# A cross-attention block on one core: the order of the last two blocks' steps, and which queue reads their inverse sums

## The chip, the core and the metric

The kernel runs on one core of one Trainium2 chip. A core has a tensor engine (PE, with its weight loads PEld), a vector engine (VectorE, DVE), a scalar engine (ScalarE, ACT), a general engine (GpSimd, POOL) and a sync engine (SyncE, SP), which issues most of the DMA transfers. Each engine works through its own instructions in the order of the program; engines wait for each other through semaphores. The metric is the device time of one execution in microseconds (us), as the median over runs.

## The reference

Sixteen pairs of an input `x` (1024 x 512) and a context (64 x 512) go through one cross-attention with a residual, all in float32. Cut to what matters:

```python
xq  = (1 + scale_q) * layernorm(x) + bias_q          # scale, bias from silu(cond) @ Wss
xkv = (1 + scale_kv) * layernorm(ctx) + bias_kv
q = (xq @ Wq + bq).reshape(B, Lq, 16, 32)
k, v = split(xkv @ Wkv + bkv)
attn = softmax(q @ k^T / sqrt(32))
out  = (attn @ v).reshape(B, Lq, 512)
return x + (out @ Wp + bp)
```

The part that matters here is the end of it: softmax, its product with `v`, and the projection by `Wp` with the residual.

## The kernel before

The rows of `x` are cut into NB = 32 blocks of 512 rows, two for each of the 16 inputs. Every block goes through the same stages, and the stages of several blocks are interleaved by hand: the program is a list of small steps, and the order of that list is the order on every engine (`manual_schedule`). Lines 1001 to 1221 bring the pipeline in, the loop from line 1224 runs blocks 4 to 29, and lines 1319 to 1413 are the way out, with y = 30 and z = 31.

For block i the steps are these:

- `scores` (L674): the products of queries and keys, in two halves of the keys, and their maxima on VectorE (L698) and copies to SBUF on ScalarE (L707).
- `maxima` and `subtract` (L734, L740): the maximum of each row is spread over a 128 x 2048 tile and taken off on Pool (L742), once for each half.
- `weights` (L746): the exponential on ScalarE (L748), in place, once for each half.
- The row sums. Up to block 30 Pool adds both halves (`total`) and VectorE sums (`row_total`, L791). Block 31 has no such addition: `sums` (L750) sums each half on VectorE (L753), and `halves_total` (L799) puts both together (L720).
- `inverse_rows` (L803): the reciprocal of the sums on VectorE (L806), a write of it to DRAM (`ltd`, L809) and four reads back (`vr`, L811), one for each group of 32 partitions. The detour changes which partition holds which row. All five transfers are issued by SP.
- `spread_rows` (L814): a transpose on VectorE (L817) that repeats each inverse sum over a 128 x 2048 tile, `vb`.
- `mix` (L839): the weights times the values on the tensor engine (L855), into two PSUM tiles of two banks.
- `divided` (L822): the result times `vb`, on VectorE, in two instructions for blocks that use the product scheme below (L835), into the tile `ot`.
- The projection by `Wp`. Block 29 does it plainly (`project`, L879, and `projected`, L893, which adds the residual and stores). All others do it with seven half-size products instead of eight. `row_sums` (L940) makes the four sums and differences of `ot` that this needs on Pool: s1 (L945, for product 5), the difference for product 7 (L946, written over a part of `ot`), s2 (L949, for product 6) and the sum for product 4 (L950, written over a part of `ot`). `product(i, n)` (L952, matmuls at L970) runs product n, eight matmuls, into a PSUM bank; `added(i, n)` (L979) adds the bank to the residual tile `r` on VectorE (L994, for block 31 L989) and stores where a part is complete.

The PSUM banks set the order around the change. The products of block 30 use banks 2 and 3, with product 2 in bank 1; those of block 31 use banks 0 and 1, with product 2 in bank 3 (`acc_bank`, L921). Products of a block add up in their bank, and `added` reads it between them, so the next product in a bank waits for the addition before it. Before the first product, `biased(i, k)` (L927) copies the projection's bias into the bank on ScalarE (L933), and for this the bank's last reader must be done: for `biased(z, 2)` that is `projected(y - 1, 3)`, for `biased(z, 3)` it is `added(y, 2)`.

The order by hand in the way out, from the last exponentials on:

```python
row_sums(y, 0)
project(y - 1, 3, later=True)
sums(z, 0)
projected(y - 1, 3)
biased(z, 2)
product(y, 1); added(y, 1)
weights(z, 1)
product(y, 2); added(y, 2)
biased(z, 3)
row_sums(y, 1)
sums(z, 1); halves_total(z); inverse_rows(z)
```

(written here with several steps on one line). After it come products 7, 6, 4 and 5 of block 30 with their additions, then `mix(z)`, `spread_rows(z)`, product 3 of block 30, `divided(z)`, `row_sums(z, 0)`, products 1 and 2 of block 31, `row_sums(z, 1)`, and products 6, 7, 5, 4 and 3 of block 31.

Of the kernel before, what the change touches and what calls it, by code (L numbers as in the profile page):

```python
# [9 lines left out]
F32 = mybir.dt.float32  # L10
AF = mybir.ActivationFunctionType
ALU = mybir.AluOpType
# [3 lines left out]
P = 128  # L16
# [4 lines left out]
def cross_attention_block(  # L21
# [51 lines left out]
    nc = tc.nc  # L73
# [10 lines left out]
    NB = B * BPB  # L84
# [661 lines left out]
    def weights(i, z):  # L746
        p = s_tiles[i, z]
        nc.scalar.activation(p, p, AF.Exp, scale=SCALE)  # L748
# [54 lines left out]
    def inverse_rows(i):  # L803

        lt = lt_tiles.pop(i)
        nc.vector.reciprocal(lt, lt)  # L806
        v = small.tile([P, NC, NJ], F32, tag="vr", name=f"vr_{i}")
        d = dram.tile([NC, 32, HPC, NJ], F32, tag="lt", name=f"ltd_{i}")
        nc.sync.dma_start(d.rearrange("c a r j -> (c a) r j"), lt)  # L809
        for r in range(HPC):  # L810
            nc.sync.dma_start(v[32 * r : 32 * r + 32], d[:, :, r, :].rearrange("c a j -> a c j"))  # L811
        vt_rows[i] = v

    def spread_rows(i):  # L814
# [78 lines left out]
    def projected(i, t):  # L893
        r = r_tiles[i]
        nc.vector.tensor_add(r[:, t, :], pp_tiles.pop((i, t)), r[:, t, :])
        nc.sync.dma_start(rows_of(out, i)[:, t, :], r[:, t, :])
        if t == NT - 1:
            r_tiles.pop(i)
# [28 lines left out]
    def biased(i, k):  # L927

        b = b_first if k == 2 else b_diff
        k = acc_bank(i, 1 if k == 2 else 7)  # L930
        acc[k] = bank(f"pp_{i}_{k}", k)
        b = b.unsqueeze(1).to_broadcast([P, 2, HO])
        nc.scalar.copy(acc[k].rearrange("p (t h) -> p t h", t=2), b)  # L933

    s1_tiles, s2_tiles = {}, {}

    def half_rows(i, m, k):
        return ot_tiles[i][:, k * HC : (k + 1) * HC, m * HT : (m + 1) * HT]

    def row_sums(i, n):  # L940

        tt = nc.gpsimd.tensor_tensor
        if n == 0:
            s1_tiles[i] = opool.tile([P, HC, HT], F32, tag="s1", name=f"s1_{i}")
            tt(s1_tiles[i], half_rows(i, 1, 0), half_rows(i, 0, 0), ALU.subtract)  # L945
            tt(half_rows(i, 1, 0), half_rows(i, 1, 1), half_rows(i, 1, 0), ALU.subtract)  # L946
        else:
            s2_tiles[i] = opool.tile([P, HC, HT], F32, tag="s2", name=f"s2_{i}")
            tt(s2_tiles[i], half_rows(i, 1, 1), s1_tiles[i], ALU.subtract)  # L949
            tt(half_rows(i, 0, 1), half_rows(i, 0, 1), s2_tiles[i], ALU.subtract)  # L950

    def product(i, n):  # L952

        rows, cols = {
            1: (lambda: half_rows(i, 0, 0), half_weights(0, 0)),
            2: (lambda: half_rows(i, 0, 1), half_weights(1, 0)),
            3: (lambda: half_rows(i, 1, 1), WT[:, 3]),
            4: (lambda: half_rows(i, 0, 1), half_weights(1, 1)),
            5: (lambda: s1_tiles.pop(i), WT[:, 0]),
            6: (lambda: s2_tiles.pop(i), WT[:, 1]),  # L960
            7: (lambda: half_rows(i, 1, 0), WT[:, 2]),
        }[n]
        rows = rows()
        k = acc_bank(i, n)
        if n == 2:
            acc[k] = bank(f"pp_{i}_{n}", k)
        for t in range(2):
            for c in range(HC):

                nc.tensor.matmul(  # L970
                    acc[k][:, t * HO : (t + 1) * HO],
                    lhsT=rows[:, c, t * P : (t + 1) * P],
                    rhs=cols[:, c, :],
                    start=n == 2 and t == 0 and c == 0,
                    stop=c == HC - 1,
                    skip_group_check=True,
                )

    def added(i, n):  # L979

        m, o = {1: (0, 0), 2: (0, 0), 6: (0, 1), 7: (1, 1), 5: (1, 1), 4: (0, 1), 3: (1, 0)}[n]
        r = r_tiles[i][:, 2 * m : 2 * m + 2, o * HO : (o + 1) * HO]
        k = acc_bank(i, n)
        a = acc[k].rearrange("p (t h) -> p t h", t=2)
        if i == NB - 1:

            for ts in ((0,), (1,)) if n == 3 else ((0, 1),):
                ts = slice(ts[0], ts[-1] + 1)
                nc.vector.tensor_add(r[:, ts, :], a[:, ts, :], r[:, ts, :])  # L989
                if n in (2, 3, 4, 5):  # L990
                    dst = rows_of(out, i)[:, 2 * m : 2 * m + 2, o * HO : (o + 1) * HO]
                    nc.sync.dma_start(dst[:, ts, :], r[:, ts, :])
            return
        nc.vector.tensor_add(r, a, r)  # L994
        if n in (3, 4):
            nc.sync.dma_start(
                rows_of(out, i)[:, 2 * m : 2 * m + 2, :], r_tiles[i][:, 2 * m : 2 * m + 2, :]
            )
# [87 lines left out]
    queries(2, 3)  # L1086
    weights(1, 0)
    queries(3, 0, later=True)
    row_sums(0, 0)
    q_stats(4, (0, 1))  # L1090
    sums(1, 0)
    q_stats(4, (2, 3), kvb=2)
# [1 line left out]
    product(0, 1)  # L1094
    added(0, 1)
    product(0, 2)
    row_sums(0, 1)
    q_scale(4, kvb=2)
    query_weight_sums()

# [34 lines left out]
    divided(1)  # L1135
    context_hidden(2)
    queries(3, 3)
    row_sums(1, 0)
    context_features(2)
    q_stats(5, (0, 1, 2))  # L1140
    product(1, 1)
# [1 line left out]
    product(1, 2)  # L1143
    added(1, 2)
    biased(1, 3)
    row_sums(1, 1)
    q_stats(5, (3,))
    q_scale(5)
    row_total(2)
# [32 lines left out]
    turn(5, range(NT))  # L1182
    load_x(7)
    q_scale(6)
    row_sums(2, 0)
    move(5)
    query_product(4, 6)
    weights(3, 0)
# [9 lines left out]
    query_product(4, 7)  # L1198
    query_out(4, 7)
    biased(2, 3)  # L1200
    row_sums(2, 1)
    key_products(2, spare("pk_2"))
    hidden(6, range(NT))
    query_product(4, 5)
# [19 lines left out]
    for i in range(4, NB - 2):  # L1224
        a, b, n, f = i - 1, i - 2, i + 1, i + 2
        kvb = i // 4 * 2 + 2
        kv = i % 4 if kvb < B else None
        if kv == 0:
            load_context(kvb)
        scores(i, 0, crossed=True)  # L1230
        product(b, 6)
        added(b, 6)
        query_product(n, 1)
        query_seed(n)
        added(b, 7)
        scores(i, 1)
        product(b, 5)
        added(b, 5)
        maxima(i)
        subtract(i)  # L1240
        product(b, 4)
        if i + 3 < NB:
            hidden(i + 3, (0, 1, 2))
        query_product(n, 2)
        query_out(n, 2)
        product(b, 3)
        spread_rows(a)
        if i + 3 < NB:
            hidden(i + 3, (3,))
        added(b, 4)  # L1250
        added(b, 3)
        biased(a, 2)
        load_residual(i)
        mix(a)
        divided(a)
        row_sums(a, 0)
        query_product(n, 6)
        weights(i, 0)
        query_out(n, 6)
        if kv == 1:  # L1260
            context_hidden(kvb)
        scale_features(f, (0, 1))
        product(a, 1)
        if i + 4 < NB:
            q_stats(i + 4, (0,))
        added(a, 1)
        product(a, 2)
        if i + 4 < NB:
            q_stats(i + 4, (1,))
        added(a, 2)  # L1270
        weights(i, 1)
        total(i)
        query_product(n, 7)
        query_out(n, 7)
        biased(a, 3)
        scale_features(f, (2, 3))
        row_sums(a, 1)
        if kv == 1:
            context_scaled(kvb)
        if kv == 2:  # L1280
            key_products(kvb, spare(f"pk_{kvb}"))
        if kv == 3:
            value_products(kvb, spare(f"pv_{kvb}"))
        if i + 3 < NB:
            turn(i + 3, range(NT))
        if i + 5 < NB:
            load_x(i + 5)
        elif i == NB - 3:
            load_residual(NB - 1)
        query_product(n, 5)  # L1290
        query_added(n, 5)
        if i + 4 < NB:
            q_stats(i + 4, (2,))
        if kv == 1:
            context_scale(kvb)
        if kv == 2:
            key_tiles(kvb)
        if kv == 3:
            value_tiles(kvb)
        query_product(n, 4)  # L1300
        query_added(n, 4)
        if i + 4 < NB:
            q_stats(i + 4, (3,), kvb=kvb if kv == 0 else None)
        query_product(n, 3)
        query_out(n, 3)
        feature_sums(f)
        product(a, 7)
        row_total(i)
        inverse_rows(i)
        if i + 3 < NB:  # L1310
            move(i + 3)
        if i + 4 < NB:
            q_scale(i + 4, kvb=kvb if kv == 0 else None)
        if kv == 1:
            context_shift(kvb)
# [3 lines left out]
    y, z = NB - 2, NB - 1  # L1319
# [47 lines left out]
    spread_rows(y)  # L1367
    projected(y - 1, 2)
    divided(y)
    row_sums(y, 0)  # L1370
    project(y - 1, 3, later=True)
    sums(z, 0)
    projected(y - 1, 3)
    biased(z, 2)
    product(y, 1)
    added(y, 1)
    weights(z, 1)
    product(y, 2)
    added(y, 2)
    biased(z, 3)  # L1380
    row_sums(y, 1)
    sums(z, 1)
    halves_total(z)
    inverse_rows(z)
    product(y, 7)
    added(y, 7)
    product(y, 6)
# [6 lines left out]
    spread_rows(z)  # L1394
    product(y, 3)
    divided(z)
    row_sums(z, 0)
    added(y, 3)
    product(z, 1)
    added(z, 1)  # L1400
    product(z, 2)
    added(z, 2)
    row_sums(z, 1)
    product(z, 6)
    added(z, 6)
    product(z, 7)
# [47 lines left out]
```

## Time and profile before

| | |
|---|---|
| median of three runs | 1044.82 us (1042.91, 1044.82, 1045.44) |
| the profiled execution | 1045.25 us |
| its span, first to last instruction | 1043.3 us |
| busy: PE, DVE, POOL, ACT | 98%, 82%, 75%, 59% of the span |
| mean granted clock of the tensor engine | 0.998 |

The span is what the profile's times refer to; the execution's own time is 1.95 us longer. By stretches of the span:

| us from the start | what runs | PE busy | DVE busy | ACT busy | POOL busy |
|---|---|---|---|---|---|
| 0 to 26 | way in | 15.5 | 13.3 | 9.4 | 0.7 |
| 26 to 1011 | the blocks | 979.5 | 823.0 | 598.5 | 770.2 |
| 1011 to 1043.3 | the way out that the change touches | 26.8 | 18.1 | 3.0 | 10.6 |

In the third stretch no engine is busy all the time: there it is waits that count, not shares. Rows of a timeline read so: start and length in us, engine, line, operation, what it writes and reads with shapes, how many instructions are merged, and in brackets how long the engine had been idle and what ended that idle time.

### The profile page before, as it was taken

Reading aid. Unit: us, or ns where it says so; the run is one execution under the profiler, and the core shown is the slowest. Engines: PE = TensorE matmul, PEld = TensorE weight load, DVE = VectorE, ACT = ScalarE, POOL = GpSimd, SP = SyncE. Lnnn points to the kernel's source line nnn. Section 1 sums busy time; section 2 is a strip of 40 time slices with the busy share of each in tenths; the row PEclk is TensorE's granted clock in tenths of the full one; section 3 lists DMA queues with packets and bytes.
Section 4 is the critical chain, followed back from the end, with each engine's and each line's share of the span. In section 5 each row is a group of like instructions: output and inputs, shape, how many; then the busy total and the mean of one; then the engine's idle time right before and its main releaser. Section 6 shows DMA issues by size and latency. Waiting matters only on the chain.

```text
span 1043.3 us, 22968 instructions
## 1 busy us (share of the span) xinstructions
PE 1021.9 (98%) x9058; PEld 760.0 (73%) x9058; DVE 854.4 (82%) x1159; ACT 610.9 (59%) x945; POOL 781.5 (75%) x502
## 2 busy tenths in 40 slices
PE   5999999999999999999999999999999999999998
PEld 3635686778777777777777787778787778777746
DVE  5798977987788977987878878898778997776795
ACT  3666755665567655766556666567557665565530
POOL 0479795887868868888668986688876886977861
PEclk9999999999999999999999999999999999999999
DMA  9851555444454434554335454344354444335122
GB/s 341 250 162 54 150 180 154 128 136 139 154 156 143 125 117 140 166 164 132 117 112 161 154 159 133 110 139 155 137 163 118 141 141 131 102 123 161 45 87 84
DMA packets 103499, 147.63 MB, mean 142 GB/s; under 512 B 33464, under 2 KB 34640, under 8 KB 103392
## 3 DMA queue, kind: packets, MB, share of 16 engines
q1 hardware_dynamic: 102368, 144.08, 43.5%
q0 software_dynamic: 1024, 2.10, 0.9%
q8 instruction: 71, 1.16, 0.5%
q14 instruction: 36, 0.29, 0.1%
HBM read 79.02 MB, written 34.60 MB: 109 GB/s over the span
## 4 chain that ended last, share of the span: by engine, by line
PE 91%; DVE 5%; DMA 1%; ACT 1%; POOL 1%; issue 1%; SPq 0%; DVEq 0%; ACTq 0%; POOLq 0%
PE pp L970 35%; PE pq L633 33%; PE po L855 6%; PE ps L681 6%; PE pq L546 4%; PE pv L434 3%; PE pk L398 3%; DVE m L698 1%; DMA x<-in_x_dram 1%; DVE bs L263 1%; DVE ht L503 0%; POOL s L742 0%; DVE lt L791 0%; ACT s L748 0%; DVE l L753 0%
## 5 line engine op out<-in xcount | busy, mean ns | idle before, releaser
L742 POOL TENSOR_TENSOR s<-s,mb 128x2048 f32<-128x2048 f32 x62 | 281.3, 4564 | 171.3 <-DVE mb L729 167.2
L707 ACT COPY s<-ps 128x1024 f32<-128x1024 f32 x128 | 129.4, 1012 | 112.7 <-DVE m L698 69.5
L698 DVE TRANSPOSE_TENSOR_REDUCE m<-ps 128x32 f32<-128x1024 f32 x128 | 150.8, 1215 | 31.1 <-PE ps L681 29.5
L970 PE MATMUL pp<-w_p_sb,ot 128*128 128x256 f32 x744 | 171.0, 379 | 0.9 <-DVE ot L835 0.5
L994 DVE TENSOR_TENSOR r<-pp,r 128x512 f32<-128x512 f32 x210 | 136.3, 670 | 32.1 <-PE pp L970 25.0
L663 ACT ACTIVATE qt<-pq,bias_t 128x256 f32<-128x256 f32 x224 | 92.6, 464 | 116.0 <-PE pq L633 113.3
L970 PEld LDWEIGHTS pp<-w_p_sb,ot 128*128 128x128 f32 x744 | 141.0, 190 | 21.8 <-issue 1.7
L748 ACT ACTIVATE s<-s 128x2048 f32<-128x2048 f32 x64 | 122.3, 1911 | 41.8 <-POOL s L742 40.0
L786 POOL TENSOR_TENSOR sum<-s,s 128x2048 f32<-128x2048 f32 x30 | 136.2, 4541 | 5.5 <-ACT s L748 5.5
L970 PEld LDWEIGHTS pp<-WT,s 128*128 128x128 f32 x496 | 90.6, 191 | 57.0 <-issue 35.2
L970 PE MATMUL pp<-WT,s 128*128 128x256 f32 x496 | 124.2, 394 | 0.2 <-POOL s L949 0.2
L970 PE MATMUL pp<-WT,ot 128*128 128x256 f32 x496 | 117.6, 380 | 1.0 <-POOL ot L946 0.6
L633 PE MATMUL pq<-xt_sums,wq_sums 128*128 128x256 f32 x448 | 108.5, 385 | 0.0
L633 PEld LDWEIGHTS pq<-xt_sums,wq_sums 128*128 128x128 f32 x448 | 82.9, 190 | 32.8 <-issue 21.8
L633 PE MATMUL pq<-xt,wq_sums 128*128 128x256 f32 x448 | 106.6, 381 | 0.0
L633 PE MATMUL pq<-xt,w_q_sb 128*128 128x256 f32 x448 | 106.0, 379 | 0.3 <-ACT pq L645 0.3
L970 PEld LDWEIGHTS pp<-WT,ot 128*128 128x128 f32 x496 | 93.9, 190 | 16.6 <-POOL ot L946 2.3
L324 ACT ACTIVATE x<-x,rstdq 128x512 f32<-128x512 f32 x128 | 96.6, 807 | 1.9 <-DVE rstdq L294 1.9
L670 DVE TENSOR_TENSOR qt<-pq,qt 128x256 f32<-128x256 f32 x112 | 42.0, 417 | 66.5 <-PE pq L633 66.1
L633 PEld LDWEIGHTS pq<-xt,w_q_sb 128*128 128x128 f32 x448 | 85.0, 190 | 13.1 <-ACT xt L573 0.8
L263 DVE BATCH_NORM_STATS2 bs<-x 128x6 f32<-128x512 f32 x128 | 86.9, 679 | 7.3 <-DMA x<-in_x_dram 7.3
L633 PEld LDWEIGHTS pq<-xt,wq_sums 128*128 128x128 f32 x448 | 83.5, 190 | 11.9 <-issue 1.4
(128 smaller groups left out, 1583.4 us busy)
## 6 DMA issues: line engine op xcount, KB each, us to landing
x<-in_x_dram SPq DMA_DIRECT2D x32, 1024.0 KB, 5.9
r<-in_x_dram SPq DMA_DIRECT2D x32, 1024.0 KB, 5.5
out_dram<-r SPq DMA_DIRECT2D x60, 512.0 KB, 3.7
xt<-ht SPq DMA_DIRECT2D x464, 64.0 KB, 2.0
wss_q<-in_L_xcond_Wss_q_dram SPq DMA_DIRECT2D x2, 1024.0 KB, 9.1
ctx<-in_ctx_dram SPq DMA_DIRECT2D x8, 256.0 KB, 3.1
wss_kv<-in_L_xcond_Wss_kv_dram SPq DMA_DIRECT2D x2, 1024.0 KB
w_kv_sb<-in_L_xcond_Wkv_dram SPq DMA_DIRECT2D x1, 2048.0 KB
```

The source lines that it names most:

```text
L263: nc.vector.bn_stats(bs, r)
L324: nc.scalar.activation(dst, src, AF.Identity, bias=rstd[:, 1, j : j + 1], scale=rstd[:, 0, j : j + 1])
L633: nc.tensor.matmul(qa[k][:, m * HT : (m + 1) * HT].rearrange("p (g n) -> p g n", g=2), lhsT=a[:, c, m * P : (m + 1) * P], rhs=x[:, :, c, : ...
L663: nc.scalar.activation(dst, src, AF.Identity, bias=bq_t[:, o : o + 1])
L681: nc.tensor.matmul(pss[r // 2][32 * c : 32 * c + 32, r % 2, :], lhsT=kt[rows, c, z * HK : (z + 1) * HK], rhs=qt[rows, c, :], start=True, s ...
L698: nc.vector.tensor_reduce(m_tiles[i][:, z, 2 * e : 2 * e + 2, :], pss[e].rearrange("p r (j a) -> p r j a", a=32), AX.X, ALU.max, apply_tra ...
L707: nc.scalar.copy(s_sb[:, 2 * e : 2 * e + 2, :], pss[e])
L742: eng.tensor_tensor(s_tiles[i, z], s_tiles[i, z], mb_tiles[i], ALU.subtract)
L748: nc.scalar.activation(p, p, AF.Exp, scale=SCALE)
L786: nc.gpsimd.tensor_tensor(t, s_tiles[i, 0], s_tiles[i, 1], ALU.add)
L970: nc.tensor.matmul(acc[k][:, t * HO : (t + 1) * HO], lhsT=rows[:, c, t * P : (t + 1) * P], rhs=cols[:, c, :], start=n == 2 and t == 0 and ...
L994: nc.vector.tensor_add(r, a, r)
```

## The change

Five things change, all in the last two blocks:

1. In block 31, `weights(z, 1)` comes before `biased(z, 2)` in the list, so before the bias copy on ScalarE.
2. `added(y, 2)` and `biased(z, 3)` go from before `row_sums(y, 1)` to behind `inverse_rows(z)`. The addition of block 30's product 2 so stands behind the sums and the reciprocal of block 31 on VectorE, and ahead of `added(y, 7)`.
3. Of the four reads of block 31's inverse sums, the second and fourth are issued by Pool instead of SP.
4. `row_sums` takes a tuple of steps, each named by the product that it serves. For block 30 the difference for product 7 now comes before s1 (7, 1, then 6, 4). Since s1 reads the part of `ot` that the difference used to overwrite, the difference gets a tile of its own there, in a buffer of the pool `qpool` (tag "wq").
5. For block 31 s2 comes before the difference for product 7: (1, 6), then (7, 4). All other blocks keep (1, 7), then (6, 4), which is the order of before.

```diff
         for r in range(HPC):
-            nc.sync.dma_start(v[32 * r : 32 * r + 32], d[:, :, r, :].rearrange("c a j -> a c j"))
+            (nc.gpsimd if i == NB - 1 and r % 2 else nc.sync).dma_start(
+                v[32 * r : 32 * r + 32], d[:, :, r, :].rearrange("c a j -> a c j")
+            )
...
-    def row_sums(i, n):
+    def row_sums(i, steps):
         tt = nc.gpsimd.tensor_tensor
...
+        for n in steps:
+            if n == 1:
+                s1_tiles[i] = opool.tile([P, HC, HT], F32, tag="s1", name=f"s1_{i}")
+                tt(s1_tiles[i], half_rows(i, 1, 0), half_rows(i, 0, 0), ALU.subtract)
+            elif n == 7:
+                d_tiles[i] = half_rows(i, 1, 0)
+                if i == NB - 2:
+                    d_tiles[i] = qpool.tile([P, 4, HC, HT], F32, tag="wq", name=f"d_{i}")[:, 0]
+                tt(d_tiles[i], half_rows(i, 1, 1), half_rows(i, 1, 0), ALU.subtract)
+            elif n == 6:
+                s2_tiles[i] = opool.tile([P, HC, HT], F32, tag="s2", name=f"s2_{i}")
+                tt(s2_tiles[i], half_rows(i, 1, 1), s1_tiles[i], ALU.subtract)
+            else:
+                tt(half_rows(i, 0, 1), half_rows(i, 0, 1), s2_tiles[i], ALU.subtract)
...
-            7: (lambda: half_rows(i, 1, 0), WT[:, 2]),
+            7: (lambda: d_tiles.pop(i), WT[:, 2]),
...
     divided(y)
-    row_sums(y, 0)
+    row_sums(y, (7, 1))
     project(y - 1, 3, later=True)
     sums(z, 0)
     projected(y - 1, 3)
+    weights(z, 1)
     biased(z, 2)
     product(y, 1)
     added(y, 1)
-    weights(z, 1)
     product(y, 2)
-    added(y, 2)
-    biased(z, 3)
-    row_sums(y, 1)
+    row_sums(y, (6, 4))
     sums(z, 1)
     halves_total(z)
     inverse_rows(z)
+    added(y, 2)
+    biased(z, 3)
     product(y, 7)
...
     divided(z)
-    row_sums(z, 0)
+    row_sums(z, (1, 6))
     added(y, 3)
     product(z, 1)
     added(z, 1)
     product(z, 2)
     added(z, 2)
-    row_sums(z, 1)
+    row_sums(z, (7, 4))
```

## Prediction

> **What bounds the kernel now.** I read the page's share of the ending chain by engine, then that chain in order of time for the last 80 us, then the timeline of the last 70 us. The page gives the whole kernel to the tensor engine: it is busy 98% of the span and holds 91% of the chain. The diff leaves the loop over blocks 4 to 29 with the same instructions in the same order (the steps of `row_sums` are only renumbered, 0 to (1, 7) and 1 to (6, 4)), so only the end, from about 1011 us on, can move. There the chain leaves the tensor engine (columns: start, length, engine, tile, line):
>
> ```profile
> 1011.94 0.59 ACT pp L933
> 1012.53 1.85 ACT s L748
> 1014.38 0.02 issue
> 1014.40 2.32 DVE l L753
> ...
> 1017.07 0.56 DVE lt L806
> ...
> 1017.65 1.44 DMA ltd<-lt
> ...
> 1021.10 1.80 DMA vr<-ltd
> ...
> 1023.02 2.32 DVE vb L817
> ...
> 1025.44 1.24 DVE ot L835
> ...
> 1029.36 1.23 POOL s L949
> 1030.59 0.04 issue
> 1030.64 8.91 PE pp L970 x40
> ```
>
> This is block 31's way out: last exponential, row sums, their inverses through DRAM (`ltd`) and back (`vr`), their spreading, the division, the Pool sums, 40 matmuls, the last output. The reader is to see that each link looks as if a saving there were a saving at the end. The timeline shows how close the runners-up are:
>
> ```profile
> 1002.48 9.07 POOL L742 TENSOR_TENSOR s<-s,mb 128x2048 f32<-128x2048 f32 x2 [8.63 <-DVE mb L729]
> ...
> 1013.62 0.69 DVE L994 TENSOR_TENSOR r<-pp,r 128x512 f32<-128x512 f32 x1 [1.03 <-PE pp L970]
> ...
> 1017.54 1.22 DVE L994 TENSOR_TENSOR r<-pp,r 128x512 f32<-128x512 f32 x2
> ...
> 1018.32 1.96 PE L970 MATMUL pp<-w_p_sb,ot 128*128 128x256 f32 x8 [0.40 <-DVE r L994]
> ...
> 1021.94 2.35 PE L855 MATMUL po<-s,vt 32*32 32x512 f32 x64
> ...
> 1022.05 0.69 DVE L994 TENSOR_TENSOR r<-pp,r 128x512 f32<-128x512 f32 x1 [1.04 <-PE pp L970]
> ...
> 1023.02 2.31 DVE L817 STREAM_TRANSPOSE vb<-vr 128x2048 f32<-128x2048 f32 x1 [0.28 <-DMA vr<-ltd]
> ...
> 1026.71 3.72 PE L970 MATMUL pp<-w_p_sb,ot 128*128 128x256 f32 x16 [0.50 <-DVE ot L835]
> ```
>
> The line that decides is the transpose of L817: VectorE waited only 0.28 us for the DMA. Just before it, in program order, stands `added(y, 5)` (1022.05), which waits for a product of block 30. However early the inverse sums land, the transpose can't pass that addition.
>
> **1. Bias copy behind the exponential.** Pool's second subtraction ends at 1002.48 + 9.07 = 1011.55. ScalarE then has the exponential's data, but stands in `biased(z, 2)`, which waits for an addition until 1011.94; the exponential follows at 1012.47. Changed, it starts at 1011.57 and ends at 1013.49 (0.02 + 1.92), against 1014.38: 0.89 earlier. The copy's reader is product(31, 1), at 1026.71, more than ten us away: cost nothing. `biased(z, 3)` now waits for the later `added(y, 2)` (about 1017.3); nothing is queued behind it on ScalarE, and its reader, product(31, 7), comes after 1031.
>
> **2. The addition behind sums and inverse.** `added(y, 2)` ran at 1013.62 to 1014.31, in the gap before the sums: it cost nothing there, but at the new time of the sums (1013.51) it would hold them until 1014.25. Moved behind the reciprocal, it frees the sums: 1013.51 + 2.32 = 1015.83, half totals 1016.15, reciprocal 1016.73 (0.30 and 0.56 from the chain, 0.02 between). Before, the write to DRAM started at 1017.65; now at 1016.75: 0.90 gained. The price is on VectorE: the addition (0.69, of which about 0.61 counts when one follows the other, since two took 1.22) now stands ahead of `added(y, 7)`. That addition was issued at 1017.54 and is now at 1016.65 + 0.61 = 1017.26. It frees the bank that product(30, 4) waited for at 1018.32, so the tensor engine gains 1017.54 - 1017.26 = **0.28 us**, not 0.90. Products 4 and 5 of block 30 and block 31's mix follow without a gap: `added(y, 5)` moves from 1022.05 to 1021.77, and is done at about 1022.4.
>
> **3. Two queues.** The write lands 1.44 after its issue: 1018.19, plus 0.02. On SP alone the four reads took 1019.11 to 1022.90 = 3.79 us (third issue 1.10, last landing 1.80 after issue), so they would land at 1022.0, already before 1022.4. With two on SP the second is issued near 1018.6 and lands by 1020.4. So the split buys nothing as long as the other two, on Pool, land by 1022.3, 4.1 us after the write. No read of 64-byte pieces was ever issued by Pool; the nearest rows are block 2's feature moves:
>
> ```profile
> 68.08 3.98 POOL L516 DMA_DIRECT2D xt<-ht  x8
> ...
> xt<-ht POOLq DMA_DIRECT2D x8, 64.0 KB, 2.0
> ```
>
> That is 0.50 us per issue and 2.0 from issue to landing: 0.5 + 2.0 = 2.5 us, landing at 1020.7. Those moves have 32 packets each, these reads some 144 (576 small packets for four in the DMA answer for 1018.9 to 1023.1). If Pool's issue grows by 128 data packets over 32, it is 2.0 us each, and with landing 2.0 after the end of the second issue 2 x 2.0 + 2.0 = 6.0 us: 1024.2, 1.9 later than needed. The lower end is a hidden transfer, since VectorE can't start earlier. I take hidden: on SP the same reads cost less per issue than the 32-packet moves (0.42 against 0.59), so here packets don't set the issue time, and between the ends the 0.50 row is the only row of Pool's own. The Trainium skill speaks against this edit: "DMA: Bandwidth & Descriptors", "Issuing engine by pattern", puts simple loads on the hardware path, and its latency list gives about 1 us to first byte from GpSimd against 0.6. By that rule the Pool landings are 0.4 later than SP's 1.8, an estimate of 0.5 + 2.2 = 2.7 us; by the row 2.5. The trace shows both kinds of move landing in 2.0, so no gap of that size at 64 KB. Either way the landing is inside 4.1, and the sum doesn't change. Queued behind the Pool issues is block 31's first row sum, which waits for the division at 1026 anyway; on SP the next is an output store.
>
> **4. Block 30's order (7, 1), with d in its own buffer.** Pool starts at 1011.5 with the difference for product 7, so product 7 can start near 1013.5 instead of 1014.20. But product 4 waits for VectorE until 1018.0, and products 7 and 6 (1.73 each) were done before that in either order. Gain 0. The new buffer's last readers ended at about 986: no wait.
>
> **5. Block 31's order (1, 6, 7, 4).** The transpose now starts at 1022.42 instead of 1023.02, so the division's first half starts at 1024.84 and ends at 1026.05 (mix(31) starts 0.28 earlier at 1021.66 and has its first half by 1023.5: no new wait). That is **0.60** on this stretch, 0.28 from part 2 and 0.32 from the removed DMA wait and its handover. Product(31, 1) then starts at 1026.11. Before, product 6 waited until 1030.64 for the third Pool sum (L949). Now s2 is the second one: s1 1026.14 to 1027.42, s2 after the second half (1027.19) to 1028.75. Products 1 and 2, 16 matmuls at 1.73 us per eight, last until 1026.11 + 3.46 = 1029.57. Product 6 starts there instead of at 1030.64. **1.07 us** in all, of which 0.47 is this order. The difference for product 7 is there at 1030.1, needed at 1031.3.
>
> **Sum.** -0.28 - 0.32 - 0.47 = -1.07 us on the profiled execution's span of 1043.3 (1045.25 with what lies around it), so about 1042.2 and 1044.2. Taken off the median of the three runs, 1044.82, this is **1043.8**: 0.1% less. About 0.3% (3.1 us) is what a measurement of this kernel can tell from no change; so I forecast no change.
>
> **Rivals.**
> A. The forecast, 1043.8: chance 0.56.
> B. All links of the chain add up: 0.90 for the inverse, 3.79 - 2.3 = 1.5 for the split reads, 0.47 for the order: -2.87, 1041.95. For it speaks the chain, where all three are links. Against it: `added(y, 5)` stands before the transpose on VectorE, and the mix ends behind the same products. Chance 0.14, as modelled matmul ends may hide some slack.
> C. The additions behind the reciprocal take everything back except the Pool order, or the order finds the same wait in VectorE's second half: between 0 and -0.5, 1044.6. Chance 0.12.
> D. Slower: the reads on Pool. At 2.0 us per issue they land at 1024.2, the transpose starts 1.9 late, and -1.07 becomes +0.8: **1045.7**. It decides from a landing at about 1023.4, 5.2 us after the write; to be slower by 0.3% it needs 8.3 us, some 3.1 per issue. For it: packets four times as many, a queue unused since 147 us. Against: SP's issues don't grow with packets. One more danger belongs here: the skill's "SBUF — State Buffer", section "SBUF: two separate sides", has a VectorE copy in its two-port mode lock GpSimd out of descriptor writing. In 1018 to 1022 VectorE runs additions with one operand in PSUM; by the rule none blocks, and no run here shows such a block. Chance 0.18.
>
> A beyond noise and half of B give 0.10 for faster by over 0.3%; half of D, where the price is past its worked-out bound, and some noise give 0.10 for slower; 0.80 within. The runs before spread over 2.5 us, so the range is 1042.0 to 1046.0: it holds B's and D's times and leaves less than 2 in 10 outside.
>
> **What would show it.** The second exponential of block 31 starting at 1011.6 and the write of the inverse at 1016.8 (parts 1 and 2); the wait of L817 no longer on a DMA but directly behind an addition (part 3); a POOL row for the reads, near 0.5 us each; product 4 of block 30 still waiting for VectorE near 1018.0 (parts 2 and 4); the 40 last matmuls starting about 1.1 earlier, with no wait for L949's successor (part 5). Wrong it would be if L817 waits for a DMA issued by Pool, or if the time before 1011 differs between the two profiles by more than the tail.

## The result, and the profile after

The changed kernel takes 1042.43 us (median of 22 runs, 1041.30 to 1044.54) against 1045.09 (22 runs) for the one before. The ratio is 0.9983, with a 95% interval of 0.9975 to 0.9991: some 0.9 to 2.6 us less, within the 0.3% band that was forecast as no change. The forecast of 1043.8 was a ratio of 0.9990, inside that interval. The number alone, though, lies nearer to rival B's 1041.95 than to 1043.8, so it takes the profiles to tell the two apart. In a second comparison on another occasion (12 runs against 23) the ratio was 0.9988, interval 0.9977 to 0.9999.

The two profiled executions differ by more than that: their spans are 1043.3 and 1040.5, 2.8 us apart. Most of it is not the change. The third-last column of the view by stretches is the granted clock of the tensor engine. Before:

```profile
159.00:161.00 2.00, 2.00 (x18) 0.75 (x19) 1.00 (x1) 0.54 (x1) 1.74 (x5) 0.66 0.58 184
161.00:163.00 2.00, 2.00 (x6) 1.62 (x5) 1.25 (x1) 1.39 (x2) 0.31 (x2) 0.50 1.02 363
```

and in the changed kernel:

```profile
159.00:161.00 2.00, 2.00 (x22) 1.16 (x7) 0.78 (x2) 1.13 (x2) 1.36 (x5) 1.00 0.58 210
161.00:163.00 2.00, 2.00 (x11) 1.77 (x10) 2.00 (x3) 0.80 (x1) 0.00 (x0) 1.00 1.06 382
```

In the profiled execution of before the clock fell to 0.66 and 0.50 (means of 2 us each). 0.34 x 2 + 0.50 x 2 is 1.7 us of lost clock, and the subtractions on Pool, which stood 0.31 us apart in the two traces at 130 us, stand 1.96 apart at 172. This drop comes in some executions of either kernel and not in others, so spans can't be compared directly. From here on I use the **tail**: the time from the start of block 31's first subtraction on Pool (L742) to the end of the span. It was 1043.3 - 1002.48 = 40.82 before and is 1040.5 - 1000.69 = **39.81** now: 1.01 us less, where the forecast's sum was 1.07. Spans are given to 0.1 us, so a tail is good to about 0.05. Times called "in the tail" count from that start.

The timeline of the changed kernel, with the rows that answer to those shown of before (the lines of the code have moved: L820 is the transpose of L817, L981 the products of L970, L1005 the additions of L994):

```profile
1000.69 9.05 POOL L742 TENSOR_TENSOR s<-s,mb 128x2048 f32<-128x2048 f32 x2 [8.64 <-DVE mb L729]
...
1009.77 1.91 ACT L748 ACTIVATE s<-s 128x2048 f32<-128x2048 f32 x1 [2.59 <-POOL s L742]
...
1014.86 1.82 DVE L1005 TENSOR_TENSOR r<-pp,r 128x512 f32<-128x512 f32 x3
1014.97 0.33 SPq L809 DMA_DIRECT2D ltd<-lt  x1
...
1016.23 1.97 PE L981 MATMUL pp<-w_p_sb,ot 128*128 128x256 f32 x8 [0.62 <-DVE r L1005]
1016.42 0.80 SPq L812 DMA_DIRECT2D vr<-ltd  x2
1016.69 1.17 POOL L812 DMA_DIRECT2D vr<-ltd  x2 [1.79 <-DMA ltd<-lt]
...
1019.96 0.69 DVE L1005 TENSOR_TENSOR r<-pp,r 128x512 f32<-128x512 f32 x1 [1.03 <-PE pp L981]
...
1020.56 2.30 DVE L820 STREAM_TRANSPOSE vb<-vr 128x2048 f32<-128x2048 f32 x1
...
1024.34 3.69 PE L981 MATMUL pp<-w_p_sb,ot 128*128 128x256 f32 x16 [0.22 <-DVE ot L838]
...
1027.87 1.89 PE L981 MATMUL pp<-WT,s 128*128 128x256 f32 x8
```

The exponential starts when Pool's subtraction ends. Three additions now follow the reciprocal in one row (1.82 us for three), and product 4 of block 30 still waits for VectorE, 0.62 us. The transpose has no bracket: it follows the addition before it, which ends at 1020.65. The last row, block 31's product 6, has none either: it follows products 1 and 2 directly. The chain in order of time now reads

```profile
1016.69 0.59 POOL vr L812
1017.28 2.89 DMA vr<-ltd
1020.17 0.04 DVEq L820
1020.21 0.36 issue
1020.56 2.31 DVE vb L820
...
1024.34 12.34 PE pp L981 x56
```

It still runs through Pool's read, but that is not the wait: the read was in at 1020.17, and the 0.36 us of "issue" behind it is time in which VectorE worked on the addition. The last link is 56 matmuls in one piece, where before it was 40, with Pool's third sum ahead of them.

### The profile page after: what moved, and what is told of

Same layout as the page of the kernel before. It is cut to its first block, busy times and chain, and to the rows that moved or that the text cites. A ratio compares the mean times of both kernels' runs of the same rounds, so it can differ in the third digit from the quotient of the medians.

```text
span 1040.5 us, 22970 instructions
## 1 busy us (share of the span) xinstructions
PE 1019.7 (98%) x9058; PEld 760.2 (73%) x9058; DVE 854.2 (82%) x1159; ACT 610.7 (59%) x945; POOL 782.1 (75%) x504
## 3 DMA queue, kind: packets, MB, share of 16 engines
q1 hardware_dynamic: 102080, 144.06, 43.2%
q0 software_dynamic: 1088, 2.12, 0.9%
## 4 chain that ended last, share of the span: by engine, by line
PE 88%; DMA 4%; DVE 4%; ACT 1%; POOL 1%; SPq 1%; issue 1%; DVEq 0%; ACTq 0%; POOLq 0%
PE pp L981 35%; PE pq L633 33%; PE po L858 6%; PE ps L681 6%; PE pv L434 2%; PE pq L546 2%; PE pk L398 2%; DMA x<-in_x_dram 2%; DMA b_p_sb<-in_L_xcond_bp_dram 1%; POOL s L742 1%; DVE m L698 1%; DMA r<-in_x_dram 1%; DVE ht L503 0%; DVE lt L791 0%; SPq L516 0%
## 5 line engine op out<-in xcount | busy, mean ns | idle before, releaser
L742 POOL TENSOR_TENSOR s<-s,mb 128x2048 f32<-128x2048 f32 x62 | 281.2, 4559 | 170.7 <-DVE mb L729 166.6
L981 PE MATMUL pp<-w_p_sb,ot 128*128 128x256 f32 x744 | 171.0, 380 | 0.8 <-DVE r L1005 0.6
L1005 DVE TENSOR_TENSOR r<-pp,r 128x512 f32<-128x512 f32 x210 | 136.2, 670 | 30.4 <-PE pp L981 24.9
L981 PEld LDWEIGHTS pp<-w_p_sb,ot 128*128 128x128 f32 x744 | 141.3, 190 | 21.4 <-issue 2.5
L981 PEld LDWEIGHTS pp<-WT,s 128*128 128x128 f32 x496 | 89.9, 190 | 56.0 <-issue 33.2
L981 PE MATMUL pp<-WT,s 128*128 128x256 f32 x496 | 122.9, 391 | 0.1
L981 PE MATMUL pp<-WT,ot 128*128 128x256 f32 x488 | 115.6, 380 | 0.4 <-ACT pp L936 0.4
L981 PEld LDWEIGHTS pp<-WT,ot 128*128 128x128 f32 x488 | 92.6, 190 | 15.3 <-POOL ot L956 1.3
```

Source lines behind the costliest of these rows:

```text
L742: eng.tensor_tensor(s_tiles[i, z], s_tiles[i, z], mb_tiles[i], ALU.subtract)
L981: nc.tensor.matmul(acc[k][:, t * HO : (t + 1) * HO], lhsT=rows[:, c, t * P : (t + 1) * P], rhs=cols[:, c, :], start=n == 2 and t == 0 and ...
```

## The experiments

Each entry quotes what was expected before the run. All but the last two are a single profiled execution, so differences of 0.1 us in the tail say little. "Product 6" is the start of block 31's product 6 in the tail: 28.16 before, 27.18 changed. It is steadier than the tail, since after it come the same 40 matmuls and the last store, which took 12.54 to 12.81 us over all runs, the changed kernel's included.

### All four reads on SP again

```diff
-            (nc.gpsimd if i == NB - 1 and r % 2 else nc.sync).dma_start(
+            nc.sync.dma_start(
```

> The changed kernel with all four reads of block 31's inverse sums on SP again. 'Tail' is the time from the start of block 31's first subtraction on Pool (L742) to the end of the span: 40.82 us before, 39.81 changed. Theory (the split is hidden behind the addition of block 30's product 5): tail 39.8, within 0.1, and the transpose into vb still starts directly behind that addition. Rival B (the split is worth its full length on SP): tail 41.0 or more.

Tail 39.76, product 6 at 27.22: as with two queues. In the timeline:

```profile
1021.53 0.69 DVE L1005 TENSOR_TENSOR r<-pp,r 128x512 f32<-128x512 f32 x1 [1.04 <-PE pp L981]
1022.14 2.31 DVE L820 STREAM_TRANSPOSE vb<-vr 128x2048 f32<-128x2048 f32 x1
```

The transpose stands directly behind the addition of product 5. The split buys nothing here, because the earlier inverse has already hidden the reads; but only just, since they landed 4.0 us after the write, 0.12 us before the transpose (before, where it waited for them, that distance was 0.12 too).

### The split alone, on the kernel before

```diff
-            nc.sync.dma_start(
+            (nc.gpsimd if i == NB - 1 and r % 2 else nc.sync).dma_start(
```

> The kernel before with the split reads alone (second and fourth read on Pool). Tail before 40.82 us, from the start of block 31's first subtraction to the end. The prediction's price of Pool's reads (0.5 per issue, 2.0 to landing) puts them 0.9 ahead of need, and the transpose starts behind the addition of product 5: tail 40.5. The price that the changed kernel's trace shows (0.28 to begin, 0.59 per issue, 2.9 from the end of the second issue to landing: 3.76 in all) equals SP's 3.79 for four: tail 40.8, with the transpose waiting for Pool's read. Rival B (full value of the split): tail 39.3.

Tail 40.61, product 6 at 27.80: 0.36 earlier in the tail. The transpose, which before waited 0.28 us for the DMA, stands directly behind the addition; the reads took 3.5 us here and landed 0.08 us before it starts. So the split has a value where the reads are late, and that value is the 0.3 to 0.4 us up to the next wait, not 1.5. It was the same 0.3 that parts 1 and 2 take by another way, so it can be had once.

### The exponential alone, on the kernel before

```diff
+    weights(z, 1)
     biased(z, 2)
     product(y, 1)
     added(y, 1)
-    weights(z, 1)
```

> The kernel before with the last exponential alone moved ahead of the bias copy; the addition of block 30's product 2 stays ahead of the sums. Theory: the exponential ends 0.89 earlier, but the sums then wait for that addition (until 1014.25 of the profile before, instead of 1014.40), so all behind it gains 0.15: tail 40.65 (40.82 before). Rival B (a saving at a link of the chain is a saving at the end): tail 39.9.

Tail 40.86: no gain at all, although the exponential ended 0.9 earlier in the tail. The timeline shows both waits that took it:

```profile
1013.27 0.69 DVE L994 TENSOR_TENSOR r<-pp,r 128x512 f32<-128x512 f32 x1 [1.03 <-PE pp L970]
1013.88 2.30 DVE L753 TRANSPOSE_TENSOR_REDUCE l<-s 128x64 f32<-128x2048 f32 x1
...
1022.77 2.31 DVE L817 STREAM_TRANSPOSE vb<-vr 128x2048 f32<-128x2048 f32 x1 [0.56 <-DMA vr<-ltd]
```

The sums follow the addition, not the exponential. The remaining 0.2 us (the write at 14.98 in the tail instead of 15.17) went to the reads, which landed 0.3 us later after the write than in the profile of before.

### Exponential and addition together, on the kernel before

```diff
-    added(y, 2)
-    biased(z, 3)
     row_sums(y, 1)
     sums(z, 1)
     halves_total(z)
     inverse_rows(z)
+    added(y, 2)
+    biased(z, 3)
```

(besides the edit of the run before)

> The kernel before with the last exponential moved and the addition of block 30's product 2 behind the inverse (parts 1 and 2), all four reads on SP and the old Pool orders. Theory: the inverse is 0.9 earlier, product 4 of block 30 only 0.28, and the transpose, now behind the addition of product 5, 0.6 to 0.67: tail 40.15 to 40.25. Rival B: tail 39.9. Rival C (taken back by the addition in front of product 7's): tail 40.5 to 40.8.

Tail 40.10, product 6 at 27.50. Parts 1 and 2 alone give 0.72 of the 1.01 us (0.66 at product 6), with the reads on SP and the old orders on Pool. The exponential alone gave nothing; the next run asks the same of the addition.

### The addition back ahead of the sums, in the changed kernel

```diff
     product(y, 2)
+    added(y, 2)
+    biased(z, 3)
     row_sums(y, (6, 4))
...
     inverse_rows(z)
-    added(y, 2)
-    biased(z, 3)
```

> The changed kernel with the addition of block 30's product 2 and the bias copy behind it put back ahead of the sums. Theory: the sums and the inverse are 0.74 later; the bank for product 4 of block 30 is free only 0.13 later; the reads land at about 0.7 later than now and become the last to arrive at the transpose, by some 0.3: tail 40.25. Rival B (the inverse is a link of the chain for all of its time): tail 40.55. If the addition's place costs nothing: 39.8 to 39.9.

Tail 39.89, product 6 at 27.28: only 0.1 longer; the expected 40.25 did not come. The sums were 0.7 later, as expected, and so was the write (14.98 in the tail instead of 14.28). But the reads landed 3.3 us after the write, the fastest of all fourteen profiles, and were there when the transpose's turn came. Product 4's bank was free 0.1 later, and that is all that was lost. With the 3.8 us of the changed kernel's own profile the transpose would have started at about 20.25 in the tail (16.41 for the landing of the write, plus 3.76 and 0.08; an estimate) and not at 19.98, and the expected loss would have come. In the run with the exponential alone the addition has the same place and nothing is left of the gain; of what differs there, the reads (4.1 us instead of 3.3) make 0.65 at the transpose (20.63 and 19.98 in the tail), and the order of block 31's sums the rest. So what the addition's place is worth depends on the reads; above 0.1 us no run shows it in the changed kernel itself.

### Block 31's old order of sums

```diff
-    row_sums(z, (1, 6))
+    row_sums(z, (1, 7))
...
-    row_sums(z, (7, 4))
+    row_sums(z, (6, 4))
```

> The changed kernel with block 31's Pool sums in the old order (1, 7), (6, 4). Theory: product 6 of block 31 waits for s2 again, tail 40.3 (0.47 longer than 39.81). Rival C (the order finds another wait in its place): tail 39.8 to 39.9.

Tail 40.24, product 6 at 27.52, 0.34 later than in the changed kernel. The weight loads show the wait:

```profile
1027.78 1.59 PEld L981 LDWEIGHTS pp<-WT,s 128*128 128x128 f32 x8 [0.55 <-POOL s L959]
```

Pool's s2 is late again. From product 1 to product 6 of block 31 it is 3.84 us here and 3.53 in the changed kernel (also 3.84 in the run with exponential and addition together, which has the old order too). This part is worth 0.3 to 0.4 us, for no instruction more.

### Block 30's old order of sums

```diff
-    row_sums(y, (7, 1))
+    row_sums(y, (1, 7))
```

> The changed kernel with block 30's first two Pool sums in the old order (1, 7). Theory: product 7 of block 30 starts 0.7 later, but product 4 starts when VectorE has read its bank, as now: tail 39.8. Rival (the tensor engine is what is late there): tail 40.4 to 40.5.

Tail 40.01. Product 7 of block 30 starts 0.66 later (11.59 in the tail instead of 10.93), and product 4 starts where it did: 15.56 against 15.54. So the order gains nothing on the tensor engine. The 0.2 us of the tail come from the reads, which landed 4.2 us after the write here and held the transpose 0.1 (20.00 instead of 19.87), and the end after product 6 (12.69 instead of 12.63).

### All four reads on Pool

```diff
-            (nc.gpsimd if i == NB - 1 and r % 2 else nc.sync).dma_start(
+            (nc.gpsimd if i == NB - 1 else nc.sync).dma_start(
```

> The changed kernel with all four reads on Pool. Theory: 0.59 per issue and 2.9 after the last issue: landing 4 x 0.59 + 2.9 = 5.3 us after Pool begins, 1.2 later than in the changed kernel; the transpose then waits for the DMA and starts 0.8 to 0.9 later: tail 40.6 to 40.7. Rival D (2.0 us per issue): landing 4 us later or more, tail 43.

Tail 39.94, product 6 at 27.18, equal to the changed kernel. The expected 40.6 was too slow: four issues took 2.24 us, but the reads were in 4.0 us after the write, against 3.8 with two on Pool. The expectation counted one issue too many, since the 2.9 us of the changed kernel's chain run from the start of the last issue and not from its end; and from that start it took only 2.0 us here.

### The addition one step later, and ScalarE in place of Pool

```diff
     inverse_rows(z)
-    added(y, 2)
-    biased(z, 3)
     product(y, 7)
     added(y, 7)
     product(y, 6)
     added(y, 6)
+    added(y, 2)
+    biased(z, 3)
```

> The changed kernel with the addition of block 30's product 2 (and the bias copy that waits for it) moved on behind the additions of products 7 and 6. Theory: product 4 of block 30 starts 0.6 earlier, the transpose then meets the landing of Pool's reads, 0.3 to 0.4 earlier than now: tail 39.4. Rival (the reads bound it already): tail 39.8.

Tail 39.40, product 6 at 26.77: product 4 of block 30 starts 0.58 earlier (14.96 in the tail), the transpose 0.42. With the second and fourth read issued by ScalarE on top of it:

```diff
-            (nc.gpsimd if i == NB - 1 and r % 2 else nc.sync).dma_start(
+            (nc.scalar if i == NB - 1 and r % 2 else nc.sync).dma_start(
```

> As the one before, with the second and fourth read issued by ScalarE instead of Pool. Theory: two reads on each of two hardware queues land 2.3 us after the write, so the transpose stands behind the addition of product 5 again, now 0.6 to 0.9 earlier than in the changed kernel: tail 38.9 to 39.2. Rival ([...]four reads take as long as on one queue): tail 39.4.

Tail 39.50. Both queues issued at once, within 0.85 us, and the transpose waited nevertheless:

```profile
1017.23 0.80 SPq L812 DMA_DIRECT2D vr<-ltd  x2
1017.24 0.85 ACTq L812 DMA_DIRECT2D vr<-ltd  x2
...
1021.14 2.31 DVE L820 STREAM_TRANSPOSE vb<-vr 128x2048 f32<-128x2048 f32 x1 [0.28 <-DMA vr<-ltd]
```

From the landing of the write to that of the reads it took 3.7 us, as on SP alone. The expected 2.3 didn't come, and the rival's time (39.4) is the nearer one. Why two queues at once were no faster, these runs don't settle.

### The changed kernel and the later addition, timed

> The changed kernel again, timed against the one before. Theory (about 1.0 us at the end of the kernel, and an interval of lower granted clock near 160 us that comes in some executions of either kernel and costs some 1.7 us): ratio near 0.999, between 0.998 and 1.000; executions of both kernels in two groups some 2 us apart, split by the granted clock (0.998 against 0.999 and 1.000), and within each group 1.0 to 1.3 us less than before. Rival (the change also gains something ahead of 1000 us): within the groups 1.8 us or more.

> The changed kernel with the addition of block 30's product 2 behind those of products 7 and 6 (tail 39.40 in one look), timed. Theory: 0.4 us less than the changed kernel within the groups of equal clock, ratio to before near 0.9985. Rival (one look's tail was chance): equal to the changed kernel.

| | ratio to before | interval | runs at clock 0.999 or more | runs at 0.998 or less |
|---|---|---|---|---|
| before | | | 1042.74 (10) | 1044.71 (13) |
| changed | 0.9988 | 0.9977 to 0.9999 | 1041.43 (4) | 1044.12 (8) |
| addition one step later | 0.9986 | 0.9974 to 0.9997 | 1041.24 (6) | 1043.88 (6) |

(medians in us, in brackets the number of runs.) Executions do split by the clock, by 2.0 to 2.7 us, in all three kernels. Within a group the change is worth 1.3 and 0.6 us, about the tail's 1.0. With so few runs the first of these doesn't by itself exclude the 1.8 that a gain ahead of 1000 us would need. The profiles do: block 31's first subtraction starts at 1001.5 to 1002.8 us in the seven profiles with the drop near 160 us and at 999.6 to 1000.7 in the seven without it, and both groups hold variants of both kernels (the changed kernel itself: 1000.69 without, 1001.74 with). Ahead of the tail the times sort by the drop, not by the change. The tail of the changed kernel's profile was 39.86 this time. The later addition is 0.2 us below the changed kernel in both groups, less than the 0.4 of the first profile, and with so few runs not clear of noise. In its profile of this occasion the tail was 39.76: the transpose waited 0.39 us for the reads, which took 4.0 us. It beats the kernel before; that it beats the changed one is likely from its earlier product 4 (14.96 in the tail in both profiles), but not shown by the times.

## Why the prediction was right, and where it was off

- **What bounds the end.** Right. The chain's links were not worth their length. Rival B, which added them up to -2.87, is refuted by the exponential alone (0 of 0.89) and the split alone (0.36 of 1.5 at product 6). Rival C, by which nearly all but the order is taken back, is refuted by parts 1 and 2 together (0.72).
- **Parts 1 and 2.** Right to within 0.1 us. In the tail the write was expected at 1016.75 - 1002.48 = 14.27 and came at 14.28; product 4's gain of 0.28 was 0.30; the transpose's 0.60 was 0.67 (19.87 for 20.54). Alone on the kernel before they gave 0.72.
- **Part 3.** The verdict "hidden" came true, and the split adds nothing to the rest, but with little to spare. The price in it was wrong twice. Pool's reads don't have the 144 packets that SP's have: the changed kernel's software queue moved

```profile
q0 software_dynamic: 1088, 2.12, 0.9%
```

  1088 packets against 1024 before, so 64 for two reads, 32 each, as in the moves that were taken as the nearest row. So the premise of rival D's 2.0 us per issue did not hold, and the issue cost 0.59. The landing was mis-sized the other way: from the 2.0 us of those moves it was put at 2.5 after the write; the split reads took 3.3 to 4.2 over eight profiles. The profile of before could have warned: the same Pool moves that landed in 2.0 near 68 us landed in 3.5 near 32 us and in 4.9 near 140 us (medians of eight), and the prediction took the fastest. With 3.5 its own sum is 4.0, at the edge of the 4.1 that it allowed. The 1.6 us of slack that this step counted on was in truth between nothing and 0.9 (4.2 us from the landing of the write to the end of the addition ahead), and where the reads come late they do hold the transpose (0.1 us in the run with block 30's old order, and some 0.05 in the second profile of the changed kernel itself, whose reads took 4.1). That the transfer was hidden at all was in part luck.
- **The rule on the software queue.** The Trainium skill's "DMA: Bandwidth & Descriptors", "Latency and other measured facts", gives the GpSimd path some 0.4 us more to the first byte. No row here shows a first byte by itself. The measured rows show Pool's first issue 0.27 after SP's (1016.69 against 1016.42), and no later landing of the whole: four reads on Pool took 4.0 us, four on SP 3.8 to 4.1. The measured total decides: within the scatter of these single profiles the queue makes no difference.
- **Part 4.** Right: nothing on the tensor engine.
- **Part 5.** Right in mechanism, a little too large: 0.47 was 0.40 between the two profiles (3.93 us from product 1 to product 6 before, 3.53 now) and 0.34 with the order alone put back. The step counted 16 matmuls at 3.46 us; they took 1027.87 - 1024.34 = 3.53 us.
- **The total.** -1.07 predicted, -1.01 in the tail: 0.58 up to product 1 of block 31 (0.60 predicted) and 0.40 from there to product 6 (0.47), the rest behind it. The further 1.8 us between the two profiles is in the main the clock's drop near 160 us in the one of before. The medians differ by 2.66 in the first comparison and by 0.71 in the second, because the share of executions with the slower clock moves them: for the changed kernel it was 9 of 22 and then 8 of 12, for the one before 13 of 23 in the second (in the first its clocks are not on record, but 13 of its 22 times lie above a gap from 1043.82 to 1044.82). That the measured 1042.43 lies 1.4 us under the forecast's 1043.8 fits this, and points to no step of the prediction.
- **Its signs of being wrong.** Two of them came up. The time ahead of the tail differs by 1.79 us, more than the tail itself; the clock's drop, which the prediction did not know of, accounts for most of it. And in the second profile of the changed kernel the transpose does stand on a read issued by Pool, for the 0.05 us named above.

## What to carry to other kernels

A link of the chain is worth its slack to the next arrival and no more: look for the instruction in program order just ahead of the one that waits, because on an in-order engine it stands there whatever the wait becomes. Two edits that remove the same wait pay once (earlier inverse, split reads), and an edit may pay nothing until its neighbour is out of the way (the exponential without the addition). Where a change sits in the last 40 us of 1040, time it by the distance between two events of the trace that enclose it; the rest of the execution brought more difference than the change. Where two arrivals lie within some tenths of a us, as the reads and the addition do here, one profile isn't enough: the kernel with the later addition had a tail of 39.40 in one and of 39.76 in the other.

## What was not expected of the hardware

- The tensor engine's granted clock drops to about half for some 3.4 us near 159 to 163 us, right after a stretch in which it stood still for about 1.2 us. It does so in seven of the fourteen profiles, with variants of both kernels among them; the seven have a mean clock of 0.998 or less, the others of 0.999 or more. It costs about 1.7 us of clock, and the two groups of runs, some 2 us apart, go with it. The Trainium skill, "TensorE: Matmul & The Clock Gate", Part 1, has a gate that halves the clock by activity in free-running windows of some 3.4 us, so that the moment differs from run to run. Half the clock for 3.4 us is 1.7 us (an estimate from the page's window), which agrees with the rows above. The page asks for an idle window of that length; here the engine stood for only 1.2 us, which doesn't fit; what counts as idle, no run here shows.
- Reading back 32 KB in pieces of 64 bytes takes 3.3 to 4.2 us from the landing of its write to its own: 3.3 to 4.2 on SP and Pool (eight profiles), 3.7 on SP and ScalarE (one), 4.0 on Pool alone (one), 3.8 to 4.1 on SP alone (four). The scatter of one variant is as large as the difference between them.
- The same read is 144 packets from SP and 32 from Pool: with two reads moved to Pool the hardware queue of the whole kernel has 288 packets less (102080 for 102368) and the software queue 64 more, with all four moved 576 less and 128 more.
